# Layer 0 of a two-layer transformer kernel: expert tiles, block products, token loads and bias sums moved to other places of the schedule

## The chip, the core and the metric

The kernel runs on one core of a Trainium2 chip. The core has five engines that work side by side, each through its own list of instructions in order: TensorE (PE in the profile; its weight loads, PEld, overlap its products), VectorE (DVE), ScalarE (ACT), GpSimd (POOL) and SyncE (SP), which issues transfers. GpSimd issues transfers too, indirect ones among them, whose rows are given by a list of indices. An engine goes on to its next instruction only when the one in front has what it waits for. The metric is the time of one execution in microseconds (us).

## The reference

The input is x, 8 batches of 512 tokens of 256 features, all in f32. Two layers follow each other; in both a modulation of each batch gives a shift, a scale and a gate ahead of and behind the two branches. Only layer 0 is touched by the change.

```python
# layer 0, attention: 16 heads of 16 features, a state M (16x16) for each batch and head
q = l2_normalize(silu(h @ Wq.T)); k = l2_normalize(silu(h @ Wk.T)); v = silu(h @ Wv.T)
beta = sigmoid(h @ Wbeta.T)
def step(M, inp):                        # over the 512 tokens, one after the other
    q_t, k_t, v_t, b_t = inp
    out_t = einsum('bnh,bnhd->bnd', q_t, M)
    delta = v_t - einsum('bnhd,bnd->bnh', M, k_t)
    M = M + b_t[..., None, None] * einsum('bnh,bnd->bnhd', k_t, delta)
    return (M, out_t)
out = out / rms * rms_weight;  x = x + ga * (out @ Wo.T)
# layer 0, experts: each token goes to one of 8 (256 -> 1024 -> 256)
top_idx = argmax(h @ gate_w.T + gate_b + expert_bias, axis=-1)
for e in range(8):
    y = relu(h @ w1[e] + b1[e]) @ w2[e] + b2[e]
    out = out + (top_idx == e)[..., None] * y
x = x + gb * out
```

Layer 1 is an ordinary causal softmax attention with 16 heads and a position bias, and a mixture of 8 experts of 256x256 with softmax weights.

## The kernel before

Layer 0 is worked in four tiles of 128 tokens (of each of the 8 batches, 1024 tokens in all). `scan(i, K, V)` runs the recurrence of tile i on VectorE: 128 steps, one for each token, of some six instructions each (L760 to L794), with the 8 x 16 = 128 pairs of batch and head on the partitions. A scan's steps follow each other and can't be shortened by other engines. The four scans come one behind the other, and all other work of layer 0 is placed among their steps, one tile earlier or later. While scan i runs, the program holds

- the rest of tile i-1, `follow(i - 1, ...)`: its attention from the deltas that the scan left (`attend`), its choice of experts (`route`) and its experts (`experts`);
- the beginning of tile i+1, `front(i + 1, 47)`: loads of x, normalization, projections to q, k and v, and the transposes to K and V that scan i+1 begins with (`heads`).

`run(pieces, scan)` sorts all these pieces by a step number and lets the program issue each piece when the scan has come to that step. The step holds for VectorE alone: there the piece's instructions stand behind the step's last one in VectorE's list. On the other engines a scheduler sets the order from the same sequence of pieces and from what depends on what. So on VectorE an instruction of a piece that is not ready holds up the scan, in order; on TensorE, ScalarE, GpSimd and SyncE work goes ahead as soon as what stands in front of it in the list is done.

`front`: for each pair p of batches, `stats(p)` loads xt (two buffers) and has ScalarE form mean, variance and their root sda (one buffer); `normal(p)` has VectorE take the reciprocal rsa (L541); then, for each batch, `turn` (ScalarE's normalized xna, transposes on TensorE, hT), `project` (L559, L563) and `squares`; for each half, `roots` and `scales`; at the end `heads` for K and for V (L704, L712). Behind the last load SyncE issues the zero fill of hs, 1.92 MB, the table into which routing scatters the rows of the slot tiles.

`attend`: for batch b, transposes at step 4b, `scores` at 4b+2, `mask` at 4b+5, `weigh` at 4b+8, `project` at 4b+10. For all tiles but the last, `weigh` also issues the block product, two matmuls (L924) whose result `state(b)` at 4b+12 masks on VectorE (dm, L970, or bdM, L967) and adds to the state that carries over between tiles. `roots`, `rest` and `stats` follow for each half of the batches (ms, L974).

`route`: normalizations and gate products for the 1024 tokens, then the choice. VectorE forms `pick`; TensorE counts it (`pc`, L1114); VectorE copies `count`; TensorE sums it (`pr`, L1121 to L1126); VectorE makes from it `over` (L1134), the slot of each token and `idx`, the rows of weights of each slot tile (L1167). GpSimd then scatters the 1024 rows into hs, eight transfers (L1173).

`experts`: the 1024 tokens, sorted by expert, fill at most 15 slot tiles (NSLOT) of 128 rows. A slot tile j takes two indirect transfers of weights issued by GpSimd (`fetch`, L1192, 1.05 and 1.18 MB), one load of its rows issued by SyncE (hslot), 32 matmuls (L1238) with relu on ScalarE (L1247), and 16 matmuls (L1259). Its result is copied from PSUM by ScalarE (L1270), the bias is added by GpSimd (L1271), and GpSimd issues the write to ys (L1272). The weights have two buffers for each part, ysb two. The gathers of the results (L1284), their product with the gate on GpSimd (L1319) and their addition to x by transfer (L1320) stand one or two tiles later.

Where the 15 slot tiles stand is written out by hand in `follow`. For tiles 0 and 1, 11 are placed in the scan that also routes (from step 70 on, one every 4.6 steps) and four in the next scan, at steps 8, 22, 40 and 62. For tile 2, 12 and three, these behind the last scan. Tile 3's attention, routing and 15 slot tiles all come behind the last scan.

```python
pieces += [(34, begin), (42, more), (51, more), (57, more), (60, more), (62, settle)]
    NT - 2: (12, 4.3, [(43, 62.1), (62.2, 62.4), (62.5, 62.7)]),
}.get(i, (11, 4.6, [(8, 11), (22, 25), (40, 43), (62.2, 62.7)]))
pieces += [(62.3, on), (62.6, on)]
        pieces.append((70 + pace * (j + half / 2), on))
```

## Time and profile before

| what | us |
|---|---|
| median of three runs | 2047.46 (2042.61 to 2047.56) |
| the profiled execution | 2056.27, span 2054.6 |
| scan 0, 1, 2, 3 begin | 55.4, 278.1, 520.2, 780.3 |
| last update of the state in scan 3 | 1008.0 |
| attention of the last tile begins on TensorE | 1026.6 |
| last tile's expert tiles end on TensorE | 1264.9 |
| layer 1 | about 1288 to 2054 |

Busy over the whole span: TensorE 1659.3 us (81%), VectorE 1526.3 (74%), ScalarE 1072.4 (52%), GpSimd 639.2 (31%). The mean clock granted to TensorE is 0.896 of full speed. The shares are means over stretches that are limited by different engines, so they are to be read stretch by stretch. A scan's begin is the start of its first reduction (kept<-terms) on VectorE. In a timeline, a row gives the start, the busy time, the engine, the line and what is written from what; in brackets stand the idle time of the engine ahead of it and what ended it.

### The profile page before, as it was taken

What the parts mean: (1) busy time and instruction counts of PE and PEld (TensorE: products, weight loads), DVE (VectorE), ACT (ScalarE), POOL (GpSimd) and SP (SyncE); (2) the same over time, 40 slices, a digit from 0 to 9 for tenths busy, and PEclk for the clock granted to TensorE, in tenths of its full rate; (3) what the DMA queues carried; (4) which work ended last, traced back from release to release, by engine and by line L of the source; (5) the groups of instructions that cost most, each with busy time, mean ns of one, the idle gap of its engine ahead of it and who ended that gap; (6) DMA issues with size and microseconds to landing.
All of it is one profiled execution on the core that took longest, in us unless ns stands there. A gap on an engine that the chain in (4) does not pass through costs nothing. (4 is left out here: it accounts for less than half of the span.)

```text
span 2054.6 us, 33919 instructions
## 1 busy us (share of the span) xinstructions
PE 1659.3 (81%) x11394; PEld 1188.7 (58%) x11394; DVE 1526.3 (74%) x5576; ACT 1072.4 (52%) x2610; POOL 639.2 (31%) x920
## 2 busy tenths in 40 slices
PE   5433147479895898939898988999999999999998
PEld 4211135369774697739766877565555556565553
DVE  4999999989989699899653001787676767676755
ACT  4353135565565755613343334987666675766630
POOL 1223023365462554623365644010111111020121
PEclk8666576699997899969998999999999999999999
DMA  5110000268202583118874973100100010010011
GB/s 178 52 49 11 0 1 11 75 233 320 77 20 78 217 304 138 46 63 312 276 124 119 323 265 105 35 17 9 29 14 25 17 24 16 22 22 11 17 21 18
DMA packets 88783, 189.71 MB, mean 92 GB/s; under 512 B 13713, under 2 KB 67281, under 8 KB 75809
## 3 DMA queue, kind: packets, MB, share of 16 engines
q0 software_dynamic: 33648, 137.30, 20.9%
q1 hardware_dynamic: 54960, 50.24, 8.5%
q8 instruction: 90, 1.47, 0.3%
q14 instruction: 85, 0.69, 0.1%
HBM read 175.12 MB, written 36.93 MB: 103 GB/s over the span
## 5 line engine op out<-in xcount | busy, mean ns | idle before, releaser
L1525 ACT ACTIVATE pr<-pr,low 128x256 f32<-128x256 f32 (+3 forms) x512 | 251.5, 554 | 127.4 <-DVE low L1513 127.0
L1238 PE MATMUL ps<-hTs,w 128*128 128x128 f32 x1920 | 240.7, 287 | 15.1 <-DMA w<-in_wrows,idx 11.9
L1513 DVE CUSTOM_DVE_ANT_0 pr<-ps,strips 128x256 f32<-128x256 f32 (+3 forms) x512 | 219.3, 485 | 42.8 <-PE ps L1500 41.9
L1238 PEld LDWEIGHTS ps<-hTs,w 128*128 128x128 f32 x1920 | 236.3, 202 | 24.0 <-issue 17.0
L1685 PE MATMUL ps<-ew,hTd 128*128 128x512 f32 x512 | 246.2, 608 | 0.0
L1259 PE MATMUL ps<-w,act 128*128 128x256 f32 x960 | 223.6, 387 | 15.5 <-ACT act L1247 10.6
L785 DVE TENSOR_REDUCE sums<-terms 128x17 f32<-128x289 f32 x508 | 226.9, 447 | 2.6 <-DVE upd L776 2.6
L790 DVE TENSOR_TENSOR state<-state,upd 128x256 f32<-128x256 f32 x511 | 214.9, 420 | 0.3 <-DVE sums L785 0.3
L760 DVE TENSOR_TENSOR terms<-state,K 128x256 f32<-128x256 f32 x512 | 211.0, 413 | 1.1 <-DVE kept L794 0.5
L1247 ACT ACTIVATE act<-ps,w 128x128 f32<-128x128 f32 x480 | 137.0, 371 | 140.1 <-PE ps L1238 113.8
L776 DVE TENSOR_TENSOR upd<-K,kept 128x256 f32<-128x256 f32 x511 | 208.8, 409 | 0.0
L1259 PEld LDWEIGHTS ps<-w,act 128*128 128x128 f32 x960 | 181.1, 194 | 41.9 <-ACT act L1247 13.4
L1690 DVE SCALAR_TENSOR_TENSOR accd<-ps,wtd,accd 128x256 f32<-128x256 f32 x256 | 123.2, 481 | 75.2 <-PE ps L1685 66.4
L1538 PEld LDWEIGHTS ps<-cst,pr 128*128 128x128 f32 x1280 | 146.1, 144 | 42.0 <-issue 28.7
L1538 PE MATMUL ps<-cst,pr 128*128 128x128 f32 x1280 | 162.7, 278 | 1.6 <-DVE low L1513 1.1
L1695 POOL TENSOR_TENSOR accd<-accd,bc_g 128x256 f32<-128x256 f32 x28 | 20.3, 724 | 448.2 <-DVE accd L1690 441.0
L1192 POOL DMA_INDIRECT w<-in_wrows,idx x120 | 123.6, 1030 | 100.4 <-ACT hTs L1216 38.7
L1685 PEld LDWEIGHTS ps<-ew,hTd 128*128 128x128 f32 x512 | 89.2, 191 | 98.2 <-issue 75.8
L794 DVE SCALAR_TENSOR_TENSOR kept<-kept,sums 128x16 f32<-128x16 f32 x508 | 117.2, 231 | 0.6 <-DVE state L790 0.6
L1546 DVE COPY prT<-ps 128x384 f32<-128x384 f32 (+1 forms) x192 | 110.2, 592 | 5.0 <-PE ps L1538 4.4
L1500 PE MATMUL ps<-kT,qTc 32*128 32x128 f32 (+3 forms) x1024 | 106.1, 470 | 5.4 <-ACT prT L1544 2.3
L1544 ACT COPY prT<-ps 128x384 f32<-128x384 f32 (+1 forms) x192 | 92.1, 507 | 18.6 <-PE ps L1538 17.3
(303 smaller groups left out, 3090.1 us busy)
## 6 DMA issues: line engine op xcount, KB each, us to landing
hs<-zero SPq DMA_DIRECT2D x4, 1920.0 KB
hslot<-hs SPq DMA_DIRECT2D x60, 128.0 KB
ys<-ysb POOLq DMA_DIRECT2D x59, 128.0 KB
x<-in_x SPq DMA_DIRECT2D x32, 128.0 KB
strips<-strip_d SPq DMA_DIRECT2D x16, 256.0 KB
out<-accd POOLq DMA_DIRECT2D x32, 128.0 KB
wm<-in_wmod SPq DMA_DIRECT2D x4, 768.0 KB
xt<-in_x SPq DMA_DIRECT2D x12, 256.0 KB
```

Of the source, the lines that this page charges most:

```text
L760: nc.vector.tensor_mul(term[:, :HD, :HD], M, K[:, s, :].unsqueeze(1).to_broadcast([P, HD, HD]))
L776: nc.vector.tensor_mul(upd, K[:, s, :].unsqueeze(2).to_broadcast([P, HD, HD]), delta(s).unsqueeze(1).to_broadcast([P, HD, HD]),)
L785: nc.vector.tensor_reduce(sums, term, AX.X, ALU.add)
L790: done = nc.vector.tensor_sub(M, M, upd)
L1192: issued["fetch"] = nc.gpsimd.indirect_dma_start(out=w, out_offset=None, in_=t[f"wrows{part}"], in_offset=bass.IndirectOffsetOnAxis(ap=idx ...
L1238: nc.tensor.matmul(ph[:, q * P : (q + 1) * P], w[:, k * FF + f * P : k * FF + (f + 1) * P], hT[:, k, :], start=(k == 0), stop=(k == 1),)
L1247: nc.scalar.activation(act[:, f, :], ph[:, q * P : (q + 1) * P], AF.Relu, bias=w[:, 2 * FF + f : 2 * FF + f + 1],)
L1259: nc.tensor.matmul(py[:, :D], act[:, f, :], w[:, f * D : (f + 1) * D], start=(f == 0), stop=(f == NFC - 1),)
L1513: nc.vector.tensor_tensor_reduce(out=pr[:, at[i]], in0=pscs[r][:, at[i]], in1=strips[:, n, S - (i + 1) * P :], scale=1.0, scalar=3.0e38, o ...
L1525: nc.scalar.activation(pr, pr, AF.Exp, bias=low, scale=-1.0)
L1538: made = nc.tensor.transpose(pt[:, n * P : (n + 1) * P], prs[r, i][:, j * P : (j + 1) * P], ident)
L1685: nc.tensor.matmul(pe, hT[0][:, k, cols], ew[:, k, e : e + 2, :], start=(k == 0), stop=(k == 1),)
```

## The change

Five things change, all in layer 0.

1. `front`: the load of a pair's tokens becomes a piece of its own, 4 steps ahead of its statistics (12 for the second pair). Pairs follow each other at 9 steps instead of 8, the reciprocal stands 10 steps behind the statistics instead of 6, and all that follows moves along; the transposes to K and V go from 55 and 58 steps behind the front's start to 62 and 65.
2. `attend`: the block product becomes a piece of its own at step 4b+14, the update of the state goes from 4b+12 to 4b+18, and the three kinds of pieces behind attention go one or two steps later.
3. The routing's later pieces go to steps 51, 59, 63 and 66 for tiles 0 to 2, and the slot tiles in the tile's own scan begin at step 77 instead of 70.
4. Tiles 0 and 1 keep 9 slot tiles in their own scan and give six to the next, at steps 42 + 4.2k (first half) and 44.1 + 4.2k (second half). Tile 2 keeps 11 and gives four to the time behind the scans.
5. Behind the scans, the bias of every slot tile is added by VectorE straight from PSUM, and SyncE issues the write to ys. The product of tile 2's gathered rows with the gate goes from GpSimd to VectorE.

```diff
@@ -501,12 +501,22 @@
                     zero.unsqueeze(1).to_broadcast([P, 2 * NSLOT, P]),
                 )
-            def stats(p):
-                xt = ep.tile([P, 2, D], F32, tag="xt", name=f"xt{i}_{p}", bufs=2)
-                load = nc.sync.dma_start(
+            def load(p):
+                xt = got[p] = ep.tile([P, 2, D], F32, tag="xt", name=f"xt{i}_{p}", bufs=2)
+                entry = nc.sync.dma_start(
                     xt,
                     t["x"][2 * p : 2 * p + 2, i * P : (i + 1) * P, :].rearrange("b p d -> p b d"),
                 )
+                if p == B // 2 - 1:
+
+                    with tc.issue_after(entry.ins):
+                        nc.sync.dma_start(
+                            hs_d[i].rearrange("(p j) (c d) -> p (j c) d", p=P, c=2),
+                            zero.unsqueeze(1).to_broadcast([P, 2 * NSLOT, P]),
+                        )
+
+            def stats(p):
+                xt = got[p]
                 mv = ep.tile([P, 2, 2], F32, tag="mva", name=f"mva{i}_{p}", bufs=2)
                 less = bank()
@@ -524,13 +534,6 @@
                 sd = ep.tile([P, 2], F32, tag="sda", name=f"sda{i}_{p}")
                 nc.scalar.activation(sd, mv[:, :, 1], AF.Sqrt, bias=ln_eps, scale=1.0 / D)
                 got[p] = xt, mv, sd
-                if p == B // 2 - 1:
-
-                    with tc.issue_after(load.ins):
-                        nc.sync.dma_start(
-                            hs_d[i].rearrange("(p j) (c d) -> p (j c) d", p=P, c=2),
-                            zero.unsqueeze(1).to_broadcast([P, 2 * NSLOT, P]),
-                        )
             def normal(p):
                 xt, mv, sd = got[p]
@@ -728,17 +731,19 @@
                 for b in range(B):
                     p, c = divmod(b, 2)
                     if c == 0:
-                        pieces.append((at + 8 * p, lambda p=p: stats(p)))
-                        pieces.append((at + 8 * p + 6, lambda p=p: normal(p)))
-                    pieces.append((at + 8 * p + 3 * c + 6, lambda b=b: turn(b)))
-                    pieces.append((at + 8 * p + 3 * c + 7, lambda b=b: project(b)))
-                    pieces.append((at + 8 * p + 3 * c + 13, lambda b=b: squares(b)))
+                        ahead = 4 if p != 1 else 12
+                        pieces.append((at + 9 * p - ahead, lambda p=p: load(p)))
+                        pieces.append((at + 9 * p, lambda p=p: stats(p)))
+                        pieces.append((at + 9 * p + 10, lambda p=p: normal(p)))
+                    pieces.append((at + 9 * p + 3 * c + 10, lambda b=b: turn(b)))
+                    pieces.append((at + 9 * p + 3 * c + 11, lambda b=b: project(b)))
+                    pieces.append((at + 9 * p + 3 * c + 17, lambda b=b: squares(b)))
                 for h in range(B // n):
-                    last = at + 16 * h + 32
+                    last = at + 18 * h + 38
                     pieces.append((last, lambda h=h: roots(h)))
                     pieces.append((last + 2, lambda h=h: scales(h)))
-            turns = at + (55 if i else 48)
+            turns = at + (62 if i else 48)
             pieces.append((turns, lambda: heads("K", qk[:, 1], 1.0)))
             pieces.append((turns + 3, lambda: heads("V", v, -1.0)))
             got["qk"] = qk
@@ -918,16 +923,6 @@
                                 start=(i == 0 and o == 0),
                                 stop=(o == 1),
                             )
-                if i < NT - 1:
-                    pm = got["pm", b] = bank()
-                    for g in range(2):
-                        nc.tensor.matmul(
-                            pm[:, g * P : (g + 1) * P],
-                            qk[:, 1, b, g * P : (g + 1) * P],
-                            got["dtok"][:, b * NH + g * 8 : b * NH + (g + 1) * 8, :],
-                            start=True,
-                            stop=True,
-                        )
                 oT = ap.tile([P, 2, P], F32, tag="oT", name=f"oT{i}_{b}")
                 nc.scalar.copy(oT, po[:, :D].rearrange("p (g t) -> p g t", g=2))
                 sqT = ap.tile([P, 2, P], F32, tag="sqT", name=f"sqT{i}_{b}")
@@ -959,6 +954,17 @@
                     nc.scalar.activation(ms, ms, AF.Sqrt, bias=rms_eps, scale=1.0 / D)
                 got[b] = y
+            def block_product(b):
+                pm = got["pm", b] = bank()
+                for g in range(2):
+                    nc.tensor.matmul(
+                        pm[:, g * P : (g + 1) * P],
+                        qk[:, 1, b, g * P : (g + 1) * P],
+                        got["dtok"][:, b * NH + g * 8 : b * NH + (g + 1) * 8, :],
+                        start=True,
+                        stop=True,
+                    )
+
             def state(b):
                 pm = got["pm", b]
                 pmv = pm[:, :D].rearrange("p (g m) -> p g m", g=2)
@@ -1001,13 +1007,14 @@
                 later = 2 if i < NT - 1 else 0
                 pieces.append((4 * b + 6 + later, lambda b=b: weigh(b)))
                 if i < NT - 1:
-                    pieces.append((4 * b + 12, lambda b=b: state(b)))
+                    pieces.append((4 * b + 14, lambda b=b: block_product(b)))
+                    pieces.append((4 * b + 18, lambda b=b: state(b)))
                 pieces.append((4 * b + 8 + later, lambda b=b: project(b)))
             for h in range(2):
-                pieces.append((16 * h + 25, lambda h=h: roots(h)))
+                pieces.append((16 * h + 27, lambda h=h: roots(h)))
                 for b in range(4 * h, 4 * h + 4):
-                    pieces.append((13 * h + 25 + b, lambda b=b: rest(b)))
-                    pieces.append((12 * h + 30 + b, lambda b=b: stats(b)))
+                    pieces.append((13 * h + 27 + b, lambda b=b: rest(b)))
+                    pieces.append((12 * h + 31 + b, lambda b=b: stats(b)))
             return got, pieces
         def route(i, h, norms):
@@ -1262,7 +1269,7 @@
                     )
                 ysb = fp.tile([P, D], F32, tag="ysb", name=f"ysb{i}_{j}", bufs=2)
                 rows = ys_d[i][j * P : (j + 1) * P, :]
-                if (i, j) == (NT - 1, NSLOT - 1):
+                if "scanned" in issued:
                     nc.vector.tensor_add(ysb, py[:, :D], w[:, NFC * D :])
                     nc.sync.dma_start(rows, ysb)
@@ -1316,7 +1323,9 @@
                     queue.append(yr)
                 if b >= DEPTH[i]:
                     yr, k = queue.pop(0), b - DEPTH[i]
-                    nc.gpsimd.tensor_mul(yr, yr, gates[1][:, k, :])
+                    (nc.vector if i == NT - 2 else nc.gpsimd).tensor_mul(
+                        yr, yr, gates[1][:, k, :]
+                    )
                     nc.gpsimd.dma_start(x2d[k][i], yr, accum_op=ALU.add)
                 yield
@@ -1345,20 +1354,22 @@
                 with tc.issue_after(issued["attention"]):
                     on()
-            pieces += [(34, begin), (42, more), (51, more), (57, more), (60, more), (62, settle)]
+            places = (51, 57, 60, 62) if i == NT - 1 else (51, 59, 63, 66)
+            pieces += [(34, begin), (42, more)]
+            pieces += zip(places, (more, more, more, settle))
             late, pace, starts = {
                 NT - 1: (0, 4, [(10 * j, 10 * j + 3) for j in range(NSLOT)]),
-                NT - 2: (12, 4.3, [(43, 62.1), (62.2, 62.4), (62.5, 62.7)]),
-            }.get(i, (11, 4.6, [(8, 11), (22, 25), (40, 43), (62.2, 62.7)]))
-            pieces += [(62.3, on), (62.6, on)]
+                NT - 2: (11, 4.4, [(43, 61.9), (62.1, 62.2), (62.3, 62.4), (62.5, 62.7)]),
+            }.get(i, (9, 4.6, [(42 + 4.2 * k, 44.1 + 4.2 * k) for k in range(6)]))
+            pieces += [(places[-1] + 0.3, on), (places[-1] + 0.6, on)]
             rest = []
             for j in range(NSLOT):
                 for half in range(2):
                     if j < late:
-                        pieces.append((70 + pace * (j + half / 2), on))
+                        pieces.append((77 + pace * (j + half / 2), on))
                         continue
                     place = starts[j - late][half]
                     if place == 43 and half == 0:
@@ -1451,6 +1462,7 @@
                 parts, more, _ = front(i + 1, 47 if i > 0 else 30)
                 pieces = pieces + more + (later if i == 0 else [])
             run(pieces, scan(i, before["K"], before["V"]))
+        issued["scanned"] = True
         more, last, _ = follow(NT - 1, before["qk"], before["V"])
         strips = [
             (1 + p0 / 3, lambda p0=p0: load_strips(p0)) for p0 in range(0, P, COPIES)
```

## The prediction

> **What bounds the kernel now.** I read the page's slices first, to see which engine each stretch belongs to.
>
> ```profile
> PE   5433147479895898939898988999999999999998
> DVE  4999999989989699899653001787676767676755
> ```
>
> One slice is 51.4 us. From slice 2 to slice 19 VectorE is at 9: the four scans of layer 0 (55.4 to 1008.0 us). In slices 21 to 24 TensorE is at 9 and VectorE almost idle: the last tile's experts. From slice 25 on it is layer 1, with TensorE at 9. So there are three bounds, and a gain counts only where it shortens the bound of its own stretch.
>
> Next the same stretches as a table (us, then busy time and instructions of TensorE, its weight loads, VectorE, ScalarE, GpSimd; clock, DMA share, GB/s).
>
> ```profile
> 55.00:278.00 223.00, 60.48 (x208) 35.68 (x208) 217.78 (x840) 66.46 (x152) 44.45 (x101) 0.62 0.09 26
> 278.00:520.00 242.00, 186.60 (x1256) 151.47 (x1255) 225.82 (x879) 138.91 (x368) 112.10 (x173) 0.82 0.41 146
> 520.00:780.00 260.00, 218.58 (x1534) 179.91 (x1533) 227.22 (x879) 151.00 (x408) 129.38 (x197) 0.90 0.40 141
> 780.00:1008.00 228.00, 180.82 (x1391) 155.19 (x1390) 220.65 (x859) 94.24 (x280) 100.37 (x139) 0.89 0.44 155
> 1106.00:1265.00 159.00, 141.64 (x885) 128.82 (x886) 9.83 (x30) 53.67 (x180) 83.95 (x97) 0.94 0.69 232
> ```
>
> VectorE works 218 to 227 us in every scan; what differs is its idle time: 5, 16, 33 and 7 us, 61 in all. The waits of VectorE say for what (total, times, longest):
>
> ```profile
> DVE rsa L541 <- ACT sda L525: 35.0, 7, 17.4
> DVE dm L970 <- PE ps L924: 10.2, 6, 4.1
> DVE ms L974 <- ACT ms L959: 9.1, 6, 3.0
> DVE bdM L967 <- PE ps L924: 3.0, 1, 3.0
> ```
>
> 57.3 of the 61 us are these four: the reciprocal of the next tile's norm waits for ScalarE's root (35.0), the state update for the block product (13.2), the attention's statistic for its root (9.1). Set in time they are: scan 0 5.0 (all rsa); scan 1 12.7 (rsa 6.10 and 2.47, bdM 2.98, ms 1.14); scan 2 31.3 (rsa 17.36, 2.47, 1.60; dm 4.05, 1.68, 0.63; ms 2.96, 0.51); scan 3 7.3 (dm, ms). No wait stands at the start of a scan. The longest, at 695.03 us, has its root here:
>
> ```profile
> 671.38 0.37 ACT L1270 COPY ysb<-ps 128x256 f32<-128x256 f32 x1 [9.06 <-remote]
> 672.17 3.78 PE L559 MATMUL ps<-wqkv,hT 128*128 128x512 f32 x4 [10.95 <-ACT hT L146]
> 694.70 0.29 ACT L525 ACTIVATE sda<-mva,cst 128x2 f32<-128x2 f32 x1
> 695.03 0.17 DVE L541 RECIPROCAL rsa<-sda 128x2 f32<-128x2 f32 x1 [17.36 <-ACT sda L525]
> ```
>
> ScalarE works in order. An expert's copy stood 9.06 us for something that the profile calls only "remote", TensorE then 10.95 for ScalarE, and the root, behind all that, came 17.36 us after VectorE wanted it.
>
> **The change, part by part.** The sum is made against the profiled execution (2056.27 us, span 2054.6), which lies 8.8 us above the median of the three runs, 2047.46; the forecast is put on the median. A step of a scan without idle time is 1.5 to 1.75 us: in scan 2, 101.8 us for the 61 steps behind step 67.
>
> *Front spread (statistics each 9 steps instead of 8, normalization 10 steps behind them instead of 6; loads apart and earlier).* The buffer of the root is single: root p+1 follows reciprocal p, so the time allowed is 9 steps instead of 6, about 15 us for 10. That covers every rsa wait but the 17.36, of which 12 would stay if its cause came back. In the new order of the instructions the six borrowed slots stand elsewhere, and that "remote" wait is one of a kind among 59 such copies, so I take it as gone. Gain: scan 0 4.6, scan 1 8.6, scan 2 21.4. The four loads of 0.26 MB move on SyncE's queue alone, with the same order against the zero fill; no wait names xt, and I cost them at nothing. Ends: 0 (no wait goes) and 34.6.
>
> *Block product in a piece of its own, state update at 4b+18 instead of 4b+12; statistics one or two steps later.* Two matmuls for each batch, as before. Gain: scan 1 4.1, scan 2 9.8, less 1.5 for the first product behind a filled TensorE. Ends 0 and 13.9.
>
> *Six slot tiles at steps 42 to 65 of the next scan instead of four around 8, 22, 40 and 62.* A slot tile is 3.73 + 3.62 = 7.3 us of TensorE. Six are 44 us in 24 steps of 1.7 = 41 us, with norms, projections and the routing's transposes between them. TensorE begins them when attention is through, at about step 38. There scan 2, without its idle time, stands at 67 us. In the new order the routing's count comes behind four and a half slots (33 us) and some 18 us of routing, norm and projection: 67 + 51 = 118 us, and VectorE wants it at step 64, about 113. VectorE waits in order, with the whole scan behind it: 4 to 8 us for the count (TensorE's own waits of 0.5 to 1.4 us for hT come on top), 2 to 5 for the next sum (over), so 10; in scan 1, with no slots of an earlier tile, 2. Ends: 3, if TensorE's idle stretch of 12.63 us at steps 43 to 52 (waiting for the scan's own tokens) is filled, and 18. In scan 3 the same wait moves only the routing.
>
> *Routing and heads later (settle 66 instead of 62, heads 62 behind the front's start instead of 55).* What was ready early is now close. Before, from the slot list (idx) to the first slot's matmuls it took 20.2 us in scan 1 and 30.3 in scan 2 (10.95 of it the stall above); from there to the last copy of the next tile's V 80.6 and 80.2. Eight slots stand between in both orders; one projection, 2 us, now comes ahead of them. So V is there 20 + 78.5 = 98.5 us after idx. Idx now falls in step 67 (scan 1) and 70 (scan 2); with one more statistic behind it, 102 and 98.5 us of scan are left. Slack 3.5 and 0: I price the new wait at scan starts at 3 in all, ends 0 and 12 (six at each).
>
> So scans 0 to 2: -4.6 - (12.7 - 2) - (31.3 - 1.5 - 10) + 3 = -32 us.
>
> *Scan 3 and the last attention.* Its end is not what counts: TensorE was still 18.7 us in slots when the scan ended, and the last tile's attention began at 1026.6, 246.3 us after the scan's start. Now settle is done at about 132 us (124.2 before), the first slot 21 us later as at 904 to 925, and 11 slots instead of 12 at the 8.1 us that they took: 242.8. -3.5 us; ends -8 and +6 (by the routing's wait).
>
> *Behind the scans: one slot more, bias by VectorE from PSUM, ys through SyncE, product with the gate by VectorE.* From 1106 to 1265 17.5 slots took 159 us, 9.07 each, for 7.3 of matmuls. GpSimd's queue shows the rest:
>
> ```profile
> 1153.95 0.37 ACT L1270 COPY ysb<-ps 128x256 f32<-128x256 f32 x1 [2.32 <-POOL rows L1319]
> 1154.84 1.10 POOL L1271 TENSOR_TENSOR ysb<-ysb,w 128x256 f32<-128x256 f32 x1
> 1156.11 1.04 POOL L1284 DMA_INDIRECT rows<-ys,slot  x1 [0.16 <-issue]
> 1157.14 0.60 POOL L1272 DMA_DIRECT2D ys<-ysb  x1
> 1157.76 0.74 POOL L1319 TENSOR_TENSOR rows<-rows,gate 128x256 f32<-128x256 f32 x1
> 1158.67 1.06 POOL L1192 DMA_INDIRECT w<-in_wrows,idx  x1 [0.17 <-issue]
> ```
>
> Where gathers run, GpSimd issues 8 to 9 us for each slot, and the weights come last. The change takes 0.72 + 0.60 + 0.74 plus three gaps of 0.3 from it, 3 us. Lower end of a slot: 7.8, the pace inside scan 3, where no gathers run; upper end 9.07. 18.5 slots at 7.8 and 4 us for weights that wait behind eight scatters make 148; at 9.07, 168. GpSimd also waited 46.6 us of this stretch for ScalarE's copies, so it is not the whole limit: I take 154, a third of the way up. -5 us; ends -11 and +9. A slot moves 2.23 MB of weights and 0.26 of rows; from 1130 to 1220 us 311 GB/s were moved, 8.0 us for 2.49 MB, near the lower end. The Trainium skill (DMA: Bandwidth & Descriptors, Specifications) gives about 358 GB/s for one core from HBM; by it, as an estimate, the transfers of a slot take 7.0 us, matmuls would be the limit, and this term would be -20. The stretch's own mean decides, and its slices up to 433 GB/s show that 358 is no ceiling here.
>
> Layer 1's instructions stand in the same order: 0. **Sum: -32 - 3.5 - 5 = -40.5 us**, 2.0% of 2056; on the median 2007.
>
> **Rivals.**
>
> *A. Routing becomes the stop.* The six slots fill TensorE just where VectorE asks for count and over. For it: 44 us of slots in 41 us of steps. Against: 12.63 us of idle TensorE there. At 18 us in scan 2 instead of 10, 8 in scan 1 instead of 2, and +6 instead of -3.5 at the last attention: -40.5 + 8 + 6 + 9.5 = -17, 2030.
>
> *B. ScalarE's root is late again.* The "remote" wait recurs behind the scatters, 12 us of the 17.36 stay, and slot 0 and V come up to 10 us late, of which 6 are not hidden under those 12: -40.5 + 12 + 6 = -22.5, 2025. For it: the scatters and the first weights still follow each other on GpSimd, and ScalarE's order still has the last borrowed slot near them. Against: one case in 59.
>
> *C. Waits go and nothing comes in their place*, with the last experts at 7.8 us a slot: 9 us of the routing's wait, the 3 for V and 6 behind the scans fall away: -40.5 - 9 - 3 - 6 = -58, 1989. For it: the 12.63 us of idle TensorE. Against: slots at 311 GB/s already.
>
> *D. Slower: VectorE's queue in the last experts.* There VectorE takes the bias sums in order with eight gate products, each of which waits for a gather. Of such waits the profile has two, of 2.72 us (in the chain) and 5.3 (among VectorE's waits). If all eight hold the bias sums, and so the two ysb buffers and TensorE, it costs 8 x 5.3 = 42 and eats the gain; from 6 us each on, with nothing hidden, the kernel is slower: 48 - 40.5 = +8, 2055. Against: TensorE runs on through free PSUM banks, and the gathers are issued slots ahead.
>
> **How the numbers follow.** My forecast 0.45, A 0.16, B 0.10, C 0.15, D 0.10, the change without measurable effect 0.04. Where A and B meet, the time lands near no change: of their 0.26, 0.03 is counted there and 0.01 above. Low end: C, 1989. High end: A and B and half of D, 2043. The likeliest case alone: 1997 to 2018. A measurement of this kernel tells about 0.3% (6 us) from no change. Faster: 0.45 + 0.16 + 0.10 + 0.15 - 0.04 = 0.82; same: 0.04 + 0.03; slower: 0.10 + 0.01.
>
> **What would show it.** Scan starts 5, 16 and 35 us earlier; rsa below 8 us in total, dm, bdM and ms below 4; new rows "over" and "count" behind TensorE at 8 to 16; at most 12 us of waits for ScalarE's V at scan starts; GpSimd without ysb and rows products behind the scans and slots there at 7.8 to 8.5 us. I am wrong if rsa keeps over 20 us, if scan 2 is longer than 250 us, or if the stretch from the last routing to the last ys write is longer than 165.

## The result, and the profile after

The changed kernel takes 2051.48 us (median), the kernel before, on the same chips, 2046.14; the ratio is 1.0032, with a 95% interval of 1.0019 to 1.0045. It is slower by about 6 us where 40 us less were forecast. The profiled execution took 2056.63 us, its span is 2054.9.

The page's slices of the changed kernel:

```profile
PE   5433157588879898769797988999999999999998
DVE  4999999999987999889563002686676767676754
```

VectorE's stretch of 9 is whole up to slice 10, where before it had an 8 in slice 8; from then on it has other gaps than before, in slices 11, 12, 16 and 17 for 8, 11, 13 and 16. It still ends in slice 19, and layer 1 still fills slices 25 to 39.

The table of stretches shows the scans (us; busy time and instructions of TensorE, its weight loads, VectorE, ScalarE, GpSimd; clock, DMA share, GB/s):

```profile
56.00:273.00 217.00, 56.82 (x207) 33.83 (x206) 216.85 (x839) 61.16 (x148) 44.48 (x101) 0.64 0.09 27
273.00:509.00 236.00, 178.16 (x1170) 140.30 (x1169) 234.39 (x879) 130.02 (x346) 107.34 (x168) 0.80 0.39 138
509.00:759.00 250.00, 216.62 (x1510) 179.23 (x1509) 230.26 (x880) 147.38 (x404) 126.50 (x193) 0.91 0.39 139
759.00:1004.00 245.00, 198.00 (x1461) 171.24 (x1459) 222.24 (x858) 100.01 (x298) 105.58 (x144) 0.88 0.45 155
1099.00:1260.00 161.00, 145.37 (x931) 134.10 (x930) 18.30 (x49) 49.64 (x171) 56.78 (x57) 0.94 0.69 231
```

Three scans are shorter (217, 236 and 250 us instead of 222.7, 242.1 and 260.1), the last is longer: 245 instead of 228. And in the second scan VectorE is busy for 234 of 236 us, where it was busy for 226: almost no idle time is left in it, and yet it got only 6 us shorter.

VectorE's waits in the four scans and behind them:

```profile
DVE rows L1326 <- DMA rows<-ys,slot: 32.3, 6, 8.9
DVE count L1126 <- PE ps L1121: 15.7, 3, 8.9
DVE stf L996 <- POOL x L988: 14.3, 13, 2.1
DVE dm L976 <- POOL bdM L977: 6.3, 5, 2.9
DVE over L1141 <- PE ps L1133: 6.1, 3, 2.8
DVE dm L976 <- PE ps L960: 2.2, 2, 1.2
DVE ms L980 <- ACT ms L954: 1.3, 2, 1.0
```

The wait for ScalarE's root, 35.0 us before, has no row any more; the block product's and the statistic's are down from 22.3 to 4.1 (with one of bdM, 0.6). In their place stand the routing's two waits for TensorE (count, over) and two that were not there before, for GpSimd: stf, the statistics behind attention, waits for the sum of the residual, and dm for the sum of the block.

Two more profiles of the kernel before and one more of the changed kernel (the runs e_before, e_before3 and e_after2, below) allow a balance by stretch. "Idx" is VectorE's last instruction of a routing, L1167 before and L1174 after; layer 1 is counted from ScalarE's first exponential.

| us | before, the profile of the prediction | before, two more | changed, two |
|---|---|---|---|
| scan 3 starts | 780.3 | 768.7, 766.4 | 758.9, 755.1 |
| from there to idx of tile 2 | 124.0 | 125.6, 123.9 | 147.6, 147.4 |
| to the last attention on TensorE | 122.3 | 118.7, 121.7 | 113.2, 113.5 |
| to idx of tile 3 | 81.6 | 80.0, 79.6 | 79.8, 82.1 |
| to the last slot tile's end | 156.7 | 155.8, 156.4 | 160.5, 157.2 |
| to layer 1 | 17.6 | 17.9, 17.9 | 17.9, 17.9 |
| layer 1 | 772.1 | 777.1, 774.5 | 777.0, 777.4 |
| span | 2054.6 | 2043.8, 2040.4 | 2054.9, 2050.6 |

Means of two against means of two: -10.5 at the start of scan 3, then +22.7, -6.9, +1.2, +2.8, 0 and +1.4, together +10.7. The medians of the 22 executions of each say +5.3; single executions of the kernel before run from 2034 to 2050 us, so the rows are to be read for their pattern: the scans give 10, the routing of scan 3 takes 23, of which one slot tile less behind it returns 7, and the last experts take 3.

### The profile page after: what moved, and what is told of

It reads as the page before. It is cut to its first block, busy times and chain, and to the rows that moved or that the text cites. A ratio compares the mean times of both kernels' runs of the same rounds, so it can differ in the third digit from the quotient of the medians.

```text
span 2054.9 us, 33953 instructions
## 1 busy us (share of the span) xinstructions
PE 1671.6 (81%) x11394; PEld 1199.7 (58%) x11394; DVE 1547.7 (75%) x5602; ACT 1056.5 (51%) x2582; POOL 608.3 (30%) x876
## 3 DMA queue, kind: packets, MB, share of 16 engines
q0 software_dynamic: 32784, 134.94, 20.6%
## 4 chain that ended last, share of the span: by engine, by line
PE 52%; DVE 24%; issue 7%; ACT 6%; DMA 5%; POOL 4%; POOLq 0%; SPq 0%; DVEq 0%; ACTq 0%
PE ps L1697 9%; PE ps L1245 6%; PE ps L1550 6%; PE ps L1266 6%; DVE sums L790 4%; DVE state L795 4%; DVE upd L781 4%; DVE terms L765 4%; PE ps L1512 4%; PE ps L1573 3%; DMA w<-in_wrows,idx 3%; PE ps L257 2%; DVE kept L799 2%; PE ps L868 2%; PE ps L917 1%
## 5 line engine op out<-in xcount | busy, mean ns | idle before, releaser
L1525 DVE CUSTOM_DVE_ANT_0 pr<-ps,strips 128x256 f32<-128x256 f32 (+3 forms) x512 | 219.3, 485 | 44.1 <-PE ps L1512 43.3
L1266 PE MATMUL ps<-w,act 128*128 128x256 f32 x960 | 230.1, 395 | 14.4 <-ACT act L1254 7.3
L1245 PE MATMUL ps<-hTs,w 128*128 128x128 f32 x1920 | 228.8, 278 | 11.2 <-DVE ysb L1274 4.7
L1245 PEld LDWEIGHTS ps<-hTs,w 128*128 128x128 f32 x1920 | 225.8, 194 | 16.7 <-DVE ysb L1274 4.8
L765 DVE TENSOR_TENSOR terms<-state,K 128x256 f32<-128x256 f32 x512 | 213.5, 418 | 0.2
L1266 PEld LDWEIGHTS ps<-w,act 128*128 128x128 f32 x960 | 186.9, 200 | 41.0 <-ACT act L1254 8.0
L1556 ACT COPY prT<-ps 128x384 f32<-128x384 f32 (+1 forms) x192 | 92.5, 508 | 18.9 <-PE ps L1550 17.2
```

Of the source, the lines that this page charges most:

```text
L765: nc.vector.tensor_mul(term[:, :HD, :HD], M, K[:, s, :].unsqueeze(1).to_broadcast([P, HD, HD]))
L1245: nc.tensor.matmul(ph[:, q * P : (q + 1) * P], w[:, k * FF + f * P : k * FF + (f + 1) * P], hT[:, k, :], start=(k == 0), stop=(k == 1),)
L1266: nc.tensor.matmul(py[:, :D], act[:, f, :], w[:, f * D : (f + 1) * D], start=(f == 0), stop=(f == NFC - 1),)
L1525: nc.vector.tensor_tensor_reduce(out=pr[:, at[i]], in0=pscs[r][:, at[i]], in1=strips[:, n, S - (i + 1) * P :], scale=1.0, scalar=3.0e38, o ...
```

## The experiments

The changed kernel has five parts: 1 the front's spread, 2 the block product apart, 3 the routing's places, 4 the slot tiles' places (3 and 4 together are called "slots" here), 5 VectorE and SyncE behind the scans. The theory at first was that the scans' gain is real and the moved slot tiles give it back; rivals were that part 5 costs, or that the slot tiles themselves had removed the waits. Edits are shown by their main lines only. Each run's ratio is its time by that of the kernel before on the same chip, with a 95% interval.

**Part 1 alone (e_front_only).** All outside part 1 is as in before:

```diff
+                        pieces.append((at + 9 * p - ahead, lambda p=p: load(p)))
+                        pieces.append((at + 9 * p, lambda p=p: stats(p)))
+                        pieces.append((at + 9 * p + 10, lambda p=p: normal(p)))
+                    last = at + 18 * h + 38
+            turns = at + (62 if i else 48)
```

> The kernel before with part 1 of the change alone (front spread, loads apart). Theory: the spread alone takes away VectorE's waits for ScalarE's root; rsa falls from 35 us to under 8, the third scan change (start of scan 3) comes about 25 us earlier than in before, 755, and since nothing else is moved behind it, the time falls by 20 to 30 us, to 2016 to 2026. Rival: the rsa waits went because the borrowed slot tiles stand elsewhere (the remote wait of ScalarE is gone with them); then rsa stays above 15 us here and the time falls by less than 12 us.

Measured: 1.0058 (1.0034 to 1.0081), slower. The rsa waits are gone, so the rival falls. But scan 3 starts at 778.8, no gain. VectorE's waits:

```profile
DVE dm L976 <- PE ps L960: 23.4, 8, 4.9
DVE terms L761 <- ACT V L715: 13.5, 2, 7.0
DVE ss L693 <- ACT ss L689: 13.4, 2, 7.0
```

The first instruction of a scan waits 7 us for the copy of V, the scales of the new tile 7 us for their roots, in both scans. The timeline at the end of scan 1 of this kernel shows why:

```profile
508.67 3.73 PE L1245 MATMUL ps<-hTs,w 128*128 128x128 f32 x32
512.24 1.97 PE L707 MATMUL ps<-cst,v 128*128 128x128 f32 x16
513.46 3.66 ACT L715 ACTIVATE V<-ps 128x512 f32<-128x512 f32 x4
517.15 0.33 DVE L761 COPY terms<-V 128x64 f32<-128x64 f32 x2 [7.03 <-ACT V L715]
```

V's transposes (L707) stand on TensorE right behind another slot tile. The heads went from steps 102 and 105 to 109 and 112, while the slot tiles stayed at 70 + 4.6 j: in scan 1 TensorE's list now has the first halves of ten slot tiles between idx and V where it had eight (counted in the trace), and in both scans V is ready 124 us behind idx instead of 99 to 111. This is the late V that the prediction priced at 0 to 12 us; it is nil in the whole change (0.23 us) because there the slot tiles move by the same seven steps.

**Parts 1 and 2 (e_front_attend).**

```diff
+                    pieces.append((4 * b + 14, lambda b=b: block_product(b)))
+                    pieces.append((4 * b + 18, lambda b=b: state(b)))
```

> Parts 1 and 2 (front spread and block product apart). Theory: 6 to 10 us less than with part 1 alone, from the dm, bdM and ms waits (22 us in before), less new waits of VectorE for GpSimd's residual sums (stf, 14 us in the changed kernel); 2010 to 2020. Rival: GpSimd's sums are late because of this part and not because of the slot tiles; then the stf waits are as long as in the changed kernel and the time equals that of part 1 alone.

Measured: 1.0032 (1.0007 to 1.0058). In the profile scan 3 starts at 767.5, 11 us ahead of part 1 alone, and the medians of the two runs, on one chip, differ by 7 us, as expected of part 2; V and ss still wait 10.8 and 12.6 us, so the total is no gain. The rival falls: without the slot tiles VectorE's waits have no row of stf.

**Parts 1, 2 and 5 (e_no_slots).** The slot tiles and the routing as in before:

```diff
-            places = (51, 57, 60, 62) if i == NT - 1 else (51, 59, 63, 66)
+            places = (51, 57, 60, 62)
-            }.get(i, (9, 4.6, [(42 + 4.2 * k, 44.1 + 4.2 * k) for k in range(6)]))
+            }.get(i, (11, 4.6, [(8, 11), (22, 25), (40, 43), (62.2, 62.7)]))
```

> The changed kernel with the slot tiles and the routing's places of before (parts 1, 2 and 5). Theory: moving the six slot tiles is what takes the gain back, by the later routing in scan 3 (idx 147.6 us behind the scan's start instead of 124.2) and one slot tile more behind the scans; without it the last tile's attention begins 246 us behind the start of scan 3 again and the time is 25 to 35 us below before, 2010 to 2020. Rival: VectorE's queue in the last experts is the loss; then the time stays within 8 us of before here.

Measured: 1.0031 (1.0002 to 1.0060). The time is the rival's, its reason isn't: from idx to the last slot tile's end it takes 150.4 us, less than the 156 of before. What keeps the gain away is again V and ss (23.6 us). In scan 3 my first theory holds: idx is at 129.9 us and attention begins at 251.8, against 147.6 and 260.8 in the changed kernel. For the time it falls: taking the moved slot tiles out does not bring the gain. The front's spread needs the later slot tiles; without them V is late.

**All but part 5 (e_no_tail).**

```diff
-                if "scanned" in issued:
+                if (i, j) == (NT - 1, NSLOT - 1):
-                    (nc.vector if i == NT - 2 else nc.gpsimd).tensor_mul(
+                    nc.gpsimd.tensor_mul(
```

> The changed kernel without part 5 (bias by ScalarE and GpSimd again, ys through GpSimd, gate products on GpSimd). Theory: between the last list of slots and the last slot tile's end 160.5 us become 165 to 170, since GpSimd issues the weights later, so 2 to 8 us longer than the changed kernel. Rival: VectorE's in-order waits for gathers (rows, 32.3 us) delay bias sums and weights more than GpSimd's sums did; then the stretch is 150 to 156 us and the kernel is 4 to 10 us faster than the changed one.

Measured: 1.0035 (1.0010 to 1.0060); the stretch from idx to the last slot tile's end is 163.9 us, 3.4 and 6.7 more than the changed kernel's 160.5 and 157.2. The theory holds in that stretch, a bit short of its 165; the time itself doesn't tell it from the changed kernel.

**Scan 3's slot tiles back (e_scan3_old).**

```diff
+            places = (51, 57, 60, 62) if i >= NT - 2 else (51, 59, 63, 66)
+                NT - 2: (12, 4.3, [(43, 62.1), (62.2, 62.4), (62.5, 62.7)]),
+                1: (11, 4.6, [(8, 11), (22, 25), (40, 43), (62.2, 62.7)]),
+                        pieces.append(((70 if i == NT - 2 else 77) + pace * (j + half / 2), on))
```

> The changed kernel, but tile 1's slot tiles (those that fall into scan 3) and scan 3's routing stand where they stood in before; tile 0's six slot tiles in scan 2 stay as changed. Theory: six slot tiles in steps 42 to 65 make TensorE late for scan 3's routing, so the last tile's attention begins 260.8 us behind the start of scan 3 instead of 246.3, and one slot tile more, 8 us, stands behind the scans. Undone, attention begins 246 to 252 us behind the start of scan 3, no count wait above 2 us stays in scan 3, and layer 1 begins 15 to 22 us earlier than in the changed kernel (1277.9), the time 12 to 20 us below it. Rival: what is late in scan 3 is GpSimd and the block product (stf, dm), whatever the slot tiles; then attention begins after 257 us or later, and the gain is under 8 us.

Measured: 0.9998 (0.9976 to 1.0020). The waits count and over are gone from scan 3, but attention begins 265.2 us behind its start, and by the ratios the run is 7 us below the changed kernel, not 12 to 20: the theory falls. In the rival's place, by another way than it said, stands this, in the timeline of scan 3:

```profile
775.84 1.97 PE L831 MATMUL ps<-cst,V 128*128 128x128 f32 x16
...
786.48 5.47 PE L1245 MATMUL ps<-hTs,w 128*128 128x128 f32 x32
...
798.75 3.62 PE L1266 MATMUL ps<-w,act 128*128 128x256 f32 x16
...
805.32 0.71 PE L960 MATMUL ps<-dtok,qk 128*128 128x128 f32 x4
806.06 0.42 DVE L976 TENSOR_TENSOR dm<-ps,cst 128x256 f32<-128x256 f32 x1 [15.35 <-PE ps L960]
```

TensorE begins the attention of the old tile (L831) 17.2 us behind the start of scan 3, in the changed kernel 2.7: tile 1 has eleven slot tiles of its own again, but they still begin at step 77 of scan 2, and two more than in the changed kernel run on into scan 3. Then the old places at steps 8 and 11 put another slot tile ahead of the first block product, in order, and VectorE waits 15.35 us for that product. In e_no_slots, with the same places but the eleven begun at step 70, attention begins 5.8 us behind the start of scan 3 and the wait is 5.80. So this run does not tell what the old places alone cost; it shows that slot tiles ahead of a block product are paid there, as those ahead of the count are paid at the routing.

**Copies as reductions (e_reduce_copy).** In the changed kernel VectorE's copy of four tokens of V takes 0.21 us in most places and up to 3.24 in some. Its timeline, with GpSimd's scaling of the new tile's q, k and v beside it:

```profile
483.83 3.51 POOL L634 TENSOR_TENSOR qk<-qk,ss 128x256 f32<-128x256 f32 x6
484.76 3.24 DVE L761 COPY terms<-V 128x64 f32<-128x64 f32 x1
487.31 0.61 POOL L634 TENSOR_TENSOR v<-v,beta 128x256 f32<-128x256 f32 x1
487.88 0.61 POOL L634 TENSOR_TENSOR qk<-qk,ss 128x256 f32<-128x256 f32 x1
```

The copy lasts over six of GpSimd's products and ends just behind the one of v, with a last one of the run still to come. The edit:

```diff
-                    nc.vector.tensor_copy(
-                        terms[s // STEPS % 2][:, :, :HD, HD], V[:, s : s + STEPS, :]
+                    nc.vector.tensor_reduce(
+                        terms[s // STEPS % 2][:, :, :HD, HD],
+                        V[:, s : s + STEPS, :].unsqueeze(3), AX.X, ALU.add,
                     )
```

> The changed kernel with VectorE's copy of four tokens of V into the scan's terms (32 for each scan) written as a reduction over an axis of one element. Theory: the copy waits out whole runs of GpSimd's products (3.24, 3.24, 2.32 and 2.81 us instead of 0.21) because both need one port to the memory, and a reduction doesn't; all 126 then take under 0.5 us, scan 1 gets 8 to 11 us shorter and scan 2 about 3, unless another instruction of VectorE waits out the same runs. Rival: the scan is not held by the copy but by something that GpSimd's runs come with (V or the memory), and the reductions are as long, 3 us, at the same places; no change in time.

Measured: 0.9998 (0.9977 to 1.0020). The reductions of all scans take 0.27 us at most, beside runs of the same products too. In the changed kernel 28 copies began while GpSimd was at elementwise work and took 0.20 to 3.24 us, in the median 0.39; here 27 reductions began so and took 0.24 to 0.27 (counted in the traces up to 1000 us). One of them:

```profile
480.49 3.52 POOL L634 TENSOR_TENSOR qk<-qk,ss 128x256 f32<-128x256 f32 x6
...
484.55 0.61 POOL L634 TENSOR_TENSOR qk<-qk,ss 128x256 f32<-128x256 f32 x1
484.66 0.27 DVE L761 TENSOR_REDUCE terms<-V 128x64 f32<-128x64 f32 x1
```

Scan 1 falls from 235.8 to 226.5 us, 9.3, as expected. Scan 2 does not: it is 254.9 (249.9), since stf waits are longer and V is now 3.75 us late at its end. That the copy is held by GpSimd's run is shown; the gain of it was partly handed on to the next waits. By the two ratios, 0.9998 and 1.0032, the run lies some 7 us below the changed kernel.

**Statistics one step later (e_gap).**

```diff
-                    pieces.append((12 * h + 31 + b, lambda b=b: stats(b)))
+                    pieces.append((12 * h + 32 + b, lambda b=b: stats(b)))
-            pieces += [(34, begin), (42, more)]
+            pieces += [(35.5, begin), (42, more)]
```

> The changed kernel with the statistics behind attention one step later (as many steps behind GpSimd's residual sums as in before; the routing's begin at 35.5). Theory: the stf waits of VectorE for GpSimd's sums (14.3 us in the changed kernel, none in before) come from the step that the change took away between them; they fall below 7 us, the scans 2 and 3 get 5 to 8 us shorter. Rival: GpSimd itself is later here, by block sums and scores that the change has put among the residual sums; then the stf waits keep more than 10 us.

Measured: 1.0009 (0.9982 to 1.0035). The stf waits fall to 6.0 us, as expected, but dm's waits rise, for GpSimd's block sums from 6.3 to 13.2 us, for TensorE's products from 2.2 to 7.8, and scans 2 and 3 are 253.0 and 242.4 us long (249.9 and 244.7). A step more only changes who waits. That GpSimd is late there by its own work fits the changed kernel's timeline, where it stands idle for only 4.1 us from 814.6 to 833.2, but no run took work from it there, so this is not shown.

**Slots alone (e_slots_only).** By now the balance spoke for a second theory: two slot tiles go from scan 1, where TensorE has slack, to places where TensorE sets the time, and the routing of scan 3 gets late.

```diff
+            places = (51, 57, 60, 62) if i == NT - 1 else (51, 59, 63, 66)
+                NT - 2: (11, 4.4, [(43, 61.9), (62.1, 62.2), (62.3, 62.4), (62.5, 62.7)]),
+            }.get(i, (9, 4.6, [(42 + 4.2 * k, 44.1 + 4.2 * k) for k in range(6)]))
+                        pieces.append((77 + pace * (j + half / 2), on))
```

> The kernel before with parts 3 and 4 alone (six slot tiles and later routing). Second theory: the slot tiles leave scan 1, where TensorE has slack, and two of them come to stand where TensorE sets the time: one between scan 3's routing and the last attention, one behind the scans; with the routing of scan 3 some 20 us later (idx at 145 to 150 us behind its start, against 124 and 126) attention begins 257 to 263 us behind the start of scan 3 instead of 244 to 246, and the stretch from the last list of slots to the last slot tile's end is 164 us instead of 156. Layer 1 begins 15 us or more later than in the second profile of before (1266.7), and the time is 0.4 to 1% above before. Rival: it is the front's spread and the block product that cost, the slot tiles take rsa waits away; then the time is at or below before.

Measured: 1.0068 (1.0048 to 1.0088). Attention begins 261.9 us behind the start of scan 3, idx is at 146.5, the last stretch takes 164.4 us, layer 1 begins at 1287.7: the second theory by each of its numbers. Some of the rival is true too: rsa is down to 16.6 us with the front as in before (28 to 35 us in the profiles of before).

**Part 5 alone (e_tail_only).** On the kernel before:

```diff
+                if "scanned" in issued:
+                    (nc.vector if i == NT - 2 else nc.gpsimd).tensor_mul(
+        issued["scanned"] = True
```

> The kernel before with part 5 alone (VectorE adds the bias behind the scans, SyncE writes ys, VectorE multiplies the gathered rows). Second theory: from the last list of slots to the last slot tile's end 150 to 152 us, as in the two profiles with part 5 and as many slot tiles as before (150.4 and 151.4), instead of 156; the time 4 to 6 us below before (0.2 to 0.3%). Rival: those two were short for another reason (one slot tile less in flight, a clock); then 155 to 159 and no change.

Measured: 0.9999 (0.9981 to 1.0018). The stretch is 151.5 us as expected, the time is not told from before. Over all profiles, with as many slot tiles as before, it takes 150.4 to 152.2 us with part 5 (six kernels) and 153.4 to 158.9 without (four kernels, before among them); with one slot tile more 157.2 to 160.5 with part 5 and 163.9 and 164.4 without. So part 5 saves 5 us there and the slot tile costs 7 to 8. The 5 us are read from the profiles; this run's time does not show them, and its interval ends at 4 us below before.

**Part 5 and the reductions (e_tail_red), and the reductions alone (e_red_only).** The edits are the three lines above and, in both, the reduction's from e_reduce_copy, on the kernel before.

> As the run with part 5 alone, and VectorE's copy of V into the scan's terms as a reduction over one element. The copies of before take 7.6, 9.0, 10.8 and 9.3 us in the four scans, the reductions of the run with them 8.3, 8.4, 8.3 and 7.9: 0.5 us more in scan 0 and 0.6 to 2.5 less in the others, so 2 to 4 us less than with part 5 alone if nothing else takes the place.

Measured: 0.9971 (0.9952 to 0.9989), faster than before, and by the ratios than the changed kernel (1.0032).

> The kernel before with the reductions instead of VectorE's copies alone. If the copies' waits for GpSimd's runs were worth the 5.7 us by which the run with part 5 and the reductions lies below the run with part 5 alone, this one lies 3 to 6 us below before (0.15 to 0.3%); if that difference came from chance or from part 5, no change.

Measured: 0.9978 (0.9955 to 1.0000). By two pairs, this run and before, part 5 with and without them, the reductions are worth 4.5 and 5.7 us; the interval of the first just reaches no change. The instructions' own lengths say as much: all 128 reductions take 31.9 and 32.6 us in these two profiles, the copies 37.8 with part 5 alone and 36.4, 37.1 and 38.2 in the three of before. The 2 to 4 us of the expectation were too few.

**A middle way (e_mix).** The changed kernel with the reductions, and eleven slot tiles for tile 1 with the other four in the middle of scan 3:

```diff
+            places = {NT - 1: (51, 57, 60, 62), NT - 2: (51, 58, 61, 63)}.get(i, (51, 59, 63, 66))
+                NT - 2: (12, 4.3, [(43, 62.1), (62.2, 62.4), (62.5, 62.7)]),
+                1: (11, 4.6, [(42 + 4.6 * k, 44.3 + 4.6 * k) for k in range(4)]),
+                        pieces.append(((72 if i == NT - 2 else 77) + pace * (j + half / 2), on))
```

> The changed kernel with the reductions instead of copies, and for tile 1 eleven slot tiles in scan 2 and four in scan 3 (steps 42 to 58), tile 2 twelve in scan 3 and three behind; scan 3's routing at 51, 58, 61, 63. Second theory: two slot tiles less in the stretches that TensorE sets, and a routing of scan 3 some 5 steps earlier: attention 250 to 254 us behind the start of scan 3, last stretch 151 us, layer 1 begins about 1258 to 1265 and the time is 0.4 to 0.8% below before. Rival: the eleven slot tiles in scan 2 run into scan 3 and hold its block products (dm), as in the run with tile 1's old places; then attention begins after 258 us.

Measured: 0.9998 (0.9982 to 1.0015). The rival holds: attention begins 268.2 us behind the start of scan 3, with a dm wait of 10.12 us at its beginning, since TensorE begins the attention of the old tile 17.4 us behind the scan's start; and the lead of 18 us with which scan 3 starts (749.0) is gone by then. The last stretch is 152.2.

**A smaller spread (e_spread3).** On part 5 and the reductions:

```diff
-                        pieces.append((at + 8 * p + 6, lambda p=p: normal(p)))
+                        pieces.append((at + 8 * p + 9, lambda p=p: normal(p)))
-                    pieces.append((last + 2, lambda h=h: scales(h)))
+                    pieces.append((last + (2 if i == 1 else 5), lambda h=h: scales(h)))
-            turns = at + (55 if i else 48)
+            turns = at + (57 if i else 48)
```

> The run with part 5 and the reductions, and a smaller spread of the front: pairs 8 steps apart as in before, the normalization 9 steps behind the statistics instead of 6, squares and roots 3 steps later, the scales 5 steps behind their roots, heads 2 steps later. Theory: the full spread of part 1 took rsa away (27 us) and gave the same time back at the two other places where VectorE waits for ScalarE, the roots of the squares (ss, 13.4 us) and V at scan starts (13.5 us), because heads came 7 steps later than the slot tiles around them. With 2 steps, rsa falls below 8 us, ss and V together stay below 6, and the time is 5 to 12 us below the run with part 5 and the reductions (0.5 to 0.9% below before). Rival: ScalarE's lateness only moves on to ss and V whatever the number of steps; then ss and V take 12 us or more and the time is that of the run without it.

Measured: 1.0114 (1.0082 to 1.0146), the slowest of all. Neither theory came out: ss is down to 3.3, V waits 9.0, but rsa still has one wait of 10.5 us and dm has 39.8, of which 13.1 and 11.6 stand at the first block products of scans 2 and 3. Nine slot tiles, not eight, stand ahead of V here. TensorE begins the attention of the old tile, behind two slot tiles, only 13.2 and 13.1 us behind the starts of these scans, in e_tail_red 2.0 and 2.7: that makes the block products late. Why TensorE is so far behind there was not settled.

**Further profiles of the two kernels (e_before, e_before3, e_after2).**

> The kernel before once more, for its profile. Layer 1's list of instructions is the same in all kernels; its length in the profiles so far was 770 to 781 us at clocks of 0.98 to 1.00. If the changed kernels made it longer, before should lie at the lower end, 769 to 773 us; if it is chance, anywhere from 768 to 782.

> The changed kernel once more, for its profile. Second theory: the start of scan 3 again at 755 to 760 us, attention 258 to 265 us behind it, 157 to 161 us from the last list of slots to the last slot tile's end, and layer 1 begins at 1272 to 1280; if its first profile was unlucky, earlier.

> The kernel before a third time. Its two profiles differ by 11.6 us at the start of scan 3 (780.3 and 768.7) and by 15.8 us at the start of layer 1 (1282.5 and 1266.7). If the second is the usual one, scan 3 starts at 766 to 773 and layer 1 at 1264 to 1273.

Measured: see the balance by stretch above. The numbers expected of the changed kernel came (755.1, 260.9, 157.2, layer 1 at 1273.2), and so did those of the third profile of before (766.4, 1265.9). Layer 1's length is chance: 777.1 and 774.5 us in before, 770.5 to 781.2 in all profiles. The changed kernel repeats itself within 5 us. The profile on which the prediction stood was an unlucky one: its wait of 17.36 us for the root is 14.00 and 11.69 in the two others, whose scan 3 starts 12 to 14 us earlier.

## Why the prediction was wrong

**Right: the waits that go.** rsa, dm, bdM and ms, where they wait for ScalarE and TensorE, fell from 57.3 us to 4.1. Idle time of VectorE in scans 0 to 2 fell from 54.1 us to 21.5, -32.6, as forecast (-32). The waits for count and over in scan 2 were priced at 10 and measured 10.9. V, priced at 3 us, cost 0.23; it was ready 103.0 and 99.8 us behind idx where 98.5 was worked out.

**Wrong: "so scans 0 to 2: -32 us".** Of the 32.6 us less idle time, 10.5 came back as busy time: the scans are 22.1 us shorter. The copies of V took 36.2 us in the three scans instead of 27.1 (27.4 and 29.0 in the other two profiles of before), and one offset of attention 2.54 instead of 0.15, the long ones in places where GpSimd is at work. I counted waits only and took durations as fixed; e_reduce_copy shows that the copies' are not. And 17.36 us was the size of one execution's wait. I had put it down to the "remote" wait of 9.06 us ahead of it; the other two profiles have no such wait, and the root is late by 14.00 and 11.69 us there all the same. Against them the gain at the start of scan 3 is 10.5 us.

**Wrong: "Scan 3 and the last attention: -3.5 us".** This is the step that turned the sign, with 18 of the 41 us by which the sum was off. Idx was put at 132 us, attention at 242.8 behind the scan's start; measured were 147.6 and 260.8, so +14.5 against the same profile. Scan 3 has 22.6 us of waits instead of 7.3, all of them ahead of idx. The two largest rows of that stretch are

```profile
DVE stf L996 <- POOL x L988: 7.7, 6, 2.1
DVE count L1126 <- PE ps L1121: 6.1, 1, 6.1
```

and behind them come dm for GpSimd with 4.8, over with 2.8 and dm for TensorE with 1.2. I had written that there "the same wait moves only the routing", and then gave it 8 us in all for later steps and waits, where the four steps alone are 7. The 15.3 us of waits more and the 7 of steps are nearly all of the 23.6 us by which idx came later. The routing of scan 3 starts everything behind it, so each of those waits counts in full. e_slots_only shows this loss with the slot tiles and the routing's places alone (idx at 146.5, attention at 261.9), with 22.4 us of waits, in part others; e_no_slots, without them, has idx at 129.9.

**Wrong in size: "Behind the scans: -5 us".** +3.8 against the same profile, +2.8 by means of two. The mechanism was right (part 5 saves 5 us), the balance wrong: the slot tile more costs 7 to 8, and VectorE indeed waits 32.3 us for gathered rows while GpSimd's weights wait for its sums, as the waits of GpSimd in that stretch show:

```profile
POOL w L1199 <- DVE ysb L1274: 31.0, 12, 7.3
```

Rival D named this; part 5 saves its 5 us all the same, so D's 42 did not come, and how much of the gain these waits took no run shows.

**Not seen: GpSimd.** stf and dm for GpSimd are 20.6 us in sum. Part 2 moved the block sums to where the residual sums stand and took a step from between sums and statistics, but stf waits come only where the slot tiles move too: parts 1 and 2 without them have no row of stf (e_front_attend), and the slot tiles without part 2 have 0.8 us of stf and 7.5 of dm (e_slots_only). I priced each edit by what it removed and never counted GpSimd's queue there. e_gap shows that one step more does not cure it; why GpSimd is late stays open.

**Rivals.** A was the nearest (routing at TensorE), but its 9.5 us for the last attention were half of the 18 missed there, and its 14 us more in scans 1 and 2 did not come: count and over are 10.9 us in scan 2 and nil in scan 1. B (rsa stays) and C fell. That part 1 needs the later slot tiles (V) was in no rival.

**The signs.** None of the three signs of being wrong came: rsa is gone, scan 2 is 249.9 us long, just under its 250, and the last slot tile ends 160.5 us behind the last idx, under 165. No sign watched the routing of scan 3, where the largest loss was.

## What to carry to other kernels

Before counting a gain, ask which engine sets the stretch into which the work goes: of the expert tiles taken from a scan with slack, the one put behind the last routing cost its full 7 to 8 us, and those put ahead of a routing that everything follows made it late, where each wait counts in full. Where several engines work in order around one sequential loop, a wait removed shows the next one close behind it, so price the next wait at every place where that loop meets another engine, GpSimd too. Take sizes of waits from more than one execution: one profile's longest wait was a third longer than in the two others. And set a sign of being wrong on every stretch of the sum.

## What the runs showed of the hardware

A copy in VectorE, 128x64 in f32, can be held while GpSimd runs elementwise products back to back: 0.21 us became 3.24 beside such a run, and the same values by a one-element reduction took 0.27 at most. What I had not expected is the length: the copy did not wait for one product of 0.61 us, but lasted over six of them, with one more to come. The Trainium skill (SBUF — State Buffer, Who interferes with whom) states the rest: a copy can take the port pair that VectorE shares with GpSimd, a reduction can't, and an instruction with two inputs from SBUF contends with GpSimd's reads. The runs agree in each point. The scan's own products keep one input in PSUM (the state, `kept` and `keys`) and took 0.42 us beside such runs as elsewhere (L765: 0.43 at most in both); the attention's offset (L135), whose two inputs lie in SBUF, took 2.54 and 2.55 us in two places beside GpSimd's selects instead of 0.15:

```profile
830.09 2.38 POOL L885 TENSOR_SCALAR_AFFINE_SELECT stk<-stk 128x512 f32<-128x512 f32 x4
830.63 2.55 DVE L135 SCALAR_TENSOR_TENSOR offf<-mvf,rsf 128x4 f32<-128x4 f32 x1
832.45 0.71 POOL L977 TENSOR_TENSOR bdM<-bdM,dm 128x256 f32<-128x256 f32 x1
```

These lines are from the timeline of the changed kernel's scan 3. That the port is what holds them is the page's reading; the runs show who is held, beside what, and that another form of instruction isn't.
